# A GRU with a residual on one core: seven block products for eight in two gates, x products 64 columns wide, a tabled order

## The chip, the core and the metric

The kernel runs on one core of a Trainium2 chip. Such a core has a matrix engine (TensorE, PE in the profile; PEld is its weight loader), three elementwise engines (VectorE = DVE, ScalarE = ACT, GpSimd = POOL), and a sync engine (SP), which here issues most DMAs. Each engine works through its own instructions in order; semaphores hold them together. Data lie in SBUF on 128 partitions; TensorE writes to PSUM, whose banks GpSimd and the DMAs do not touch in this kernel. The metric is the device time of one execution in microseconds (us), as the median over runs.

## What is computed

A gated recurrent unit over 128 steps, 64 batch rows, 512 inputs and 512 hidden units, in float32, added to its input. After every fourth step but the last the state goes through one more layer.

```python
def step(h, inp):
    x_t, prop = inp
    comb = jnp.concatenate([x_t, h], axis=-1)
    z = jax.nn.sigmoid(comb @ Wz + bz)
    r = jax.nn.sigmoid(comb @ Wr + br)
    comb2 = jnp.concatenate([x_t, r * h], axis=-1)
    h_cand = jnp.tanh(comb2 @ Wh + bh)
    h_new = (1.0 - z) * h + z * h_cand
    h_next = jnp.where(prop, jnp.tanh(h_new @ Wp + bp), h_new)
    return (h_next, h_new)
...
return x + ys          # ys: all h_new, [64, 128, 512]
```

Each weight matrix has an upper half that meets x and a lower half that meets h. The x halves do not depend on the recurrence.

## The kernel before

**Recurrence.** The 64 batch rows are two halves of 32 (`S = 2`, `V = 32`). A gate of a half is eight matmuls: four blocks of 128 inputs, each with two matmuls of 256 columns (`products`, L213). The stationary operand is 32 columns wide (a block of the transposed state), so that each matmul takes one of TensorE's four 32-column groups: half h uses the groups 2h and 2h + 1. In PSUM, a partition stands for (half, column block, batch row), and the free axis for the other columns.

A step of a half (`half`, L777) runs: gate r; `crossed` (L239), which applies the sigmoid and brings the two column blocks onto the partitions of the state; r·h and its 32×32 transposes on VectorE (L794, L244); gate z; gate h on the transposed r·h; tanh; z·candidate, minus `keep` = (z − 1)·h (L831, L840); the transpose for the next step. ScalarE copies the x part of each gate from SBUF into PSUM ahead of the products (`seed`, L377), and the products add to it. The two halves are generators that give way to each other by the columns that they have issued, half 1 a lag of 700 columns behind half 0 (L868 to L880).

**x products.** From group 2 on (a group is four steps) the x products of four steps at once are block products by Strassen's scheme in Winograd's form, on two levels: seven for eight over (step pairs, input halves, column halves), and each of these again seven for eight. So a group takes 49 products instead of 64, each a pair of matmul rounds of 192 columns (three gates of 64). `batch` (L480 on) runs two outer products at once over five PSUM banks: ScalarE copies partial sums out (L484), VectorE adds them into a block `mb` (L501 to L511), and GpSimd adds those blocks, with the biases, into the steps' x parts `cp` (L542, L547), in the partition layout that the gates use. GpSimd also makes the sums of x (`four`, L307) and adds the new state to x for the output (L752). `fill` (L396) puts a number of x products, given per step by the tables `PLACES`, `HEAD` and `TAIL`, between the gates. Groups 0 and part of the last are plain products (`plain`).

**Order.** Within an engine it is the order in which this code issues: the two generators, the fills, and `behind_step` (L691) for the GpSimd sums, loads and stores. SyncE loads x twice in groups of four steps (`xr` for the output, `xs` for the products) and stores groups of four steps.

Of the kernel before, what the change touches and what calls it, by code (L numbers as in the profile page):

```python
# [11 lines left out]
U16 = mybir.dt.uint16  # L12
AF = mybir.ActivationFunctionType
ALU = mybir.AluOpType
PSUM = bass.MemoryType.PSUM


@with_exitstack
def kernel(
# [14 lines left out]
    nc = tc.nc  # L34
# [8 lines left out]
    K = D // P  # L43
    Q4 = 4
    CHUNK = 4
    FIRST = 2
    LAST = T // Q4 - 1
# [3 lines left out]

    const = ctx.enter_context(tc.tile_pool(name="const", bufs=1))
    xrp = ctx.enter_context(tc.tile_pool(name="xr", bufs=2))  # L60
    one = ctx.enter_context(tc.tile_pool(name="one", bufs=1))
    xtp = ctx.enter_context(tc.tile_pool(name="xt", bufs=2))
    mbp = ctx.enter_context(tc.tile_pool(name="mb", bufs=3))
    two = ctx.enter_context(tc.tile_pool(name="two", bufs=2))
# [3 lines left out]
    zeros = one.tile([P, 4 * J], BF16, tag="cq", name="zeros")  # L68
    nc.vector.memset(zeros, 0.0)
    ones = const.tile([1, V], F32, name="ones")  # L70
    nc.gpsimd.memset(ones, 1.0)

    wx = const.tile([P, K, 3, H], F32, name="wx")
    wh = [const.tile([P, K, H], F32, name=f"wh_{i}") for i in range(3)]
    wp = const.tile([P, K, H], F32, name="wp")

    tw = {n: const.tile([P, S, NQ, 3, J // 2], F32, name=f"tw_{n}") for n in (2, 3, 4, 5)}
    tf = {n: const.tile([P, NQ, 3, J // 4], F32, name=f"tf_{n}") for n in (1, 2, 3)}
    tt = const.tile([P, 7, 3, NQ, 3, J // 4], F32, name="tt")
    gates_in = (Wr, Wz, Wh)  # L80

    bias_row = tt.rearrange("p a b c d e -> p (a b c d e)")[0:1, : 3 * H].rearrange(
        "p (i n) -> p i n", i=3
    )
# [4 lines left out]
    def load_x(tile_, t0, n):  # L89
        for h in range(S):  # L90
            for q in range(NQ):
                nc.sync.dma_start(
                    out=tile_[part(q), 0:n, h, :], in_=x[ts(h, V), t0 : t0 + n, ts(q, J)]
                )

    def load_step(t, engs):
        for q in range(NQ):
            engs[q % len(engs)].dma_start(
                out=xr[0][part(q), t], in_=x[:, t, ts(q, J)].rearrange("(h b) j -> b h j", h=S)
            )  # L100

    def load_wx(wt, w, k0=0, k1=K):
        nc.sync.dma_start(  # L103
            out=wt[:, k0:k1, :], in_=w.rearrange("(p k) n -> p k n", k=K)[:, k0:k1]
        )

    def load_wh(wt, w, engs=(nc.sync,)):
        for q in range(NQ):
            engs[q % len(engs)].dma_start(  # L109
                out=wt[part(q)], in_=w[ts(q, P), :].rearrange("(k e) n -> e k n", e=V)  # L110
            )

    xr = {}

    def new_xr(g):
        xr[g] = xrp.tile([P, Q4, S, J], F32, tag="xr", name=f"xr_{g}")

    h_init = two.tile([P, S, J], F32, tag="h", name="h_init")
    bias_x = const.tile([P, C, S, 3, J // 2], F32, name="bias_x")
    bias_p = const.tile([P, S, J], F32, name="bias_p")  # L120
    new_xr(0)
    load_step(0, (nc.sync, nc.scalar))
    for k in range(0, K, 2):
        load_wx(wx[:, :, R, :], gates_in[R][:D], k, k + 2)
    for i in (Z, H_):
        load_wx(wx[:, :, i, :], gates_in[i][:D])

    load_step(1, (nc.gpsimd,))
    for i, b in enumerate((br, bh, bz)):
        nc.gpsimd.dma_start(out=bias_row[:, i, :], in_=b.rearrange("(o n) -> o n", o=1))  # L130
    for t in (2, 3):
        load_step(t, (nc.gpsimd,))
    for h in range(S):
        nc.gpsimd.dma_start(
            out=h_init[:, h, :],
            in_=h0[ts(h, V), :].rearrange("b (q j) -> q b j", q=NQ),
        )

    nc.gpsimd.tensor_copy(wh[R][0:1, 0, 0:1], wx[0:1, K - 1, H_, 0:1])
    for i in range(3):  # L140
        load_wh(wh[i], gates_in[i][D:], (nc.sync, nc.gpsimd))

    dummy = const.tile([1, 1], F32, name="dummy")
    nc.scalar.activation(dummy, ones[:, 0:1], AF.Sigmoid)

    xs = {}

    def load_xs(g):
        if g * Q4 < T:
            xs[g] = one.tile([P, Q4, S, J], F32, tag=f"xs{g % 2}", name=f"xs_{g}")  # L150
            load_x(xs[g], g * Q4, Q4)

    new_xr(1)
    load_x(xr[1], Q4, Q4)
    load_xs(2)
    load_wh(wp, Wp)
    for q in range(NQ):
        nc.sync.dma_start(
            out=bias_p[part(q)],
            in_=bp.rearrange("(o d c j) -> c o d j", o=1, d=2, c=2)[q % 2].broadcast_to(  # L160
                [V, S, J]
            ),
        )


    P_ = 3
    rec = [ps_c.tile([P, 2, 2, J], F32, name=f"rec_{n}") for n in ("0", "1", "z")]
    z = rec[2][:, 1]

    def gate_ps(i, h):  # L170
        return rec[2][:, 0] if i == Z else rec[h][:, 0 if i == R else 1]

    scratch = [ps_c.tile([P, 4 * J], F32, name=f"scratch_{n}") for n in "qraxy"]
    q_ps, r_ps, a_ps, *x_two = (
        s[:, : 3 * J].rearrange("p (m h v) -> p m h v", m=2, h=S) for s in scratch
    )
    q_bank, r_bank, a_bank, *x_banks = range(5)
    r_ = scratch[r_bank][:, 3 * J :]

    def quarters(v):  # L180
        return v.rearrange("p n (d c j) -> p c n d j", d=2, c=2)

    def spread(bank, rows, which):
        bank = bank.rearrange("p (i d j) -> p i d j", i=2, d=2)
        for h in range(S):
            for c in range(2):
                nc.tensor.matmul(
                    bank[part(2 * h + c), 0 : len(which)],
                    lhsT=ones,
                    rhs=quarters(bias_row[:, rows])[:, c],  # L190
                    start=True,
                    stop=True,
                )
        for j, i in enumerate(which):
            nc.scalar.copy(
                bias_x[:, :, :, i, :].rearrange("p n d u -> p d n u"),
                bank[:, j].rearrange("p d (n u) -> p d n u", n=C),
            )

    bias0 = bias_x[:, 0]  # L200
    bias_d = const.tile([P, S, 3, J // 2], F32, name="bias_d")

    def idle(n):
        for i in range(n):
            nc.tensor.matmul(
                rec[i // NQ % 3].rearrange("p a d n -> p (a d n)")[part(i % NQ)],
                lhsT=zeros[:, :V],
                rhs=zeros,
                start=True,
                stop=True,  # L210
            )

    def products(ps, h, left, rhs, start=False):  # L213
        for c in range(2):
            nc.tensor.matmul(  # L215
                ps[part(2 * h + c)],
                lhsT=left,
                rhs=rhs(c),
                start=start,
                stop=True,  # L220
                skip_group_check=True,
            )

    def gate(i, h, lT, w):
        for k in range(K):
            products(gate_ps(i, h), h, lT[:, h, ts(k, V)], lambda c: quarters(w)[:, c, k])
            yield S * J

    def product(ps, h, lT, w, k, start=False):
        c0, s0 = divmod(k, C)  # L230
        products(
            ps.rearrange("p (d j) -> p d j", d=2),
            h,
            lT[:, c0, s0 * B + h * V : s0 * B + (h + 1) * V],
            lambda c: quarters(w)[:, c, k],
            start,
        )

    def crossed(dst, h, i, func):  # L239
        for d in range(2):  # L240
            nc.scalar.activation(dst[ts(d, 2 * V)], gate_ps(i, h)[ts(h, 2 * V), d, :], func)  # L241

    def turn(dst, src):
        nc.vector.transpose(out=dst, in_=src)  # L244

    def new_T(tag, name):
        return two.tile([P, S, P], F32, tag=tag, name=name)

    xT = {}

    def join_x(g, i):
        if g * Q4 >= T:
            return
        if g not in xT:
            xT[g] = xtp.tile([P, Q4, C, P], F32, tag="xT", name=f"xT_{g}")
        src = xr[g] if g < FIRST else xs[g]
        nc.vector.transpose(
            out=xT[g][:, i].rearrange("p c (a h b) -> p h (c a) b", a=S, h=S),
            in_=src[:, i].rearrange("p h (e k) -> p h k e", k=K),
        )  # L260

    def outer(kb, nb, ka):
        return wx[:, kb * S + ka, :, :].rearrange("p g (q n u) -> p n q g u", q=NQ, n=C)[:, nb]

    OPERAND = {
        1: lambda ka: outer(0, 0, ka),
        2: lambda ka: outer(1, 0, ka),
        3: lambda ka: outer(1, 1, ka),
        4: lambda ka: tw[4][:, ka],
        5: lambda ka: tw[5][:, ka],  # L270
# [649 lines left out]
```

## Time and profile before

| | |
|---|---|
| median of 3 runs | 1277.04 us (1275.2 to 1277.14) |
| span of the profiled execution | 1273.0 us |
| difference of the median to that span | 4.0 us |
| mean granted TensorE clock | 0.997 of full speed |
| issues by SyncE | 767 DMAs |
| moved by DMA | 60.82 MB, mean 48 GB/s |

The span runs from the first to the last instruction of one profiled execution. A group line has: line, engine, operation, output<-inputs, output partitions × elements <- input, count | busy time in us, mean ns of one | idle time of the engine just before them, and what ended it. A matmul `128*32 128x256` has 128 rows, 32 stationary columns and 256 streamed columns. Every float32 matmul of the program is two records in the trace, each with its own weight load. Ends of matmuls are modelled by the profiler, starts are not. In a timeline a row has start, length, engine, line, operation and count; in brackets stands the engine's idle time before it.

### The profile page before, as it was taken

How to read it: one execution, taken by the hardware profiler on the slowest of the kernel's cores; microseconds unless marked ns; L12 is line 12 of the kernel's file. 1: busy time of each engine (PE TensorE's matmuls, PEld its weight loads, DVE VectorE, ACT ScalarE, POOL GpSimd, SP SyncE). 2: the span in 40 equal slices, each digit the busy share in tenths (PEclk: the TensorE clock that was granted, in tenths of full speed). 3: DMA queues.
4: the chain of work that ended last, by engine and by line, in shares of the span. 5: the costliest groups of instructions: out<-in, count | busy, mean ns of one | idle time of the engine just before them, and what ended most of it. 6: DMA issues, size and time to landing. Idle time of an engine off the chain costs nothing.

```text
span 1273.0 us, 60669 instructions
## 1 busy us (share of the span) xinstructions
PE 1255.9 (99%) x25954; PEld 1150.3 (90%) x25954; DVE 800.4 (63%) x2153; ACT 835.5 (66%) x2685; POOL 906.0 (71%) x1053
## 2 busy tenths in 40 slices
PE   7899999999999999999999999999999999999998
PEld 4699999999999999999999999999999999999885
DVE  2765666666666666666666665666666666666544
ACT  1356666766666666676666667666666666666665
POOL 8788767777677786777687677776777777677530
PEclk9999999999999999999999999999999999999999
DMA  8302212102121111211111121111111112111010
GB/s 233 76 19 53 52 41 60 40 24 49 53 53 36 36 47 42 53 36 44 49 32 53 46 59 37 29 43 53 53 37 37 48 39 52 37 52 35 4 50 21
DMA packets 112212, 60.82 MB, mean 48 GB/s; under 512 B 12776, under 2 KB 108520, under 8 KB 111944
## 3 DMA queue, kind: packets, MB, share of 16 engines
q1 hardware_dynamic: 110532, 54.71, 16.5%
q8 instruction: 205, 3.36, 1.1%
q0 software_dynamic: 1120, 2.11, 0.7%
q14 instruction: 63, 0.52, 0.1%
q10 hardware_dynamic: 292, 0.13, 0.0%
HBM read 40.11 MB, written 16.78 MB: 45 GB/s over the span
## 4 chain that ended last, share of the span: by engine, by line
PE 95%; DMA 2%; DVE 1%; issue 1%; SPq 0%; ACT 0%; POOL 0%; POOLq 0%; DVEq 0%
PE rec L215 43%; PE rec_z L215 16%; PE scratch_r L215 14%; PE scratch_q L215 10%; PE scratch_a L215 5%; PE scratch_x L215 4%; PE scratch_y L215 4%; DMA wh<-in_L_cond_Wh_dram 1%; DMA wx<-in_L_cond_Wh_dram 1%; DVE tw L292 0%; DVE tw L293 0%; DVE tw L291 0%; SPq L109 0%; ACT rec_z L241 0%; SPq L103 0%
## 5 line engine op out<-in xcount | busy, mean ns | idle before, releaser
L215 PE MATMUL rec<-wh,rhT 128*32 128x256 f32 x4096 | 373.2, 379 | 0.0
L215 PE MATMUL rec<-wh,hT 128*32 128x256 f32 x3072 | 281.1, 381 | 4.9 <-DVE hT L244 4.7
L215 PE MATMUL rec_z<-wh,hT 128*32 128x256 f32 x3072 | 280.0, 379 | 0.1
L215 PEld LDWEIGHTS rec<-wh,rhT 128*32 128x32 f32 x4096 | 241.2, 110 | 23.4 <-ACT scratch_r L241 1.3
L241 ACT ACTIVATE scratch_r<-rec 64x128 f32<-64x128 f32 x512 | 128.0, 250 | 136.0 <-PE rec L215 68.1
L380 ACT COPY rec<-cp 64x256 f32<-64x256 f32 x512 | 189.8, 371 | 23.6 <-DVE cp L418 4.2
L215 PEld LDWEIGHTS rec<-wh,hT 128*32 128x32 f32 x3072 | 175.0, 110 | 27.3 <-ACT rec L380 6.4
L215 PEld LDWEIGHTS rec_z<-wh,hT 128*32 128x32 f32 x3072 | 184.8, 110 | 7.3 <-issue 0.6
L241 ACT ACTIVATE rec_z<-rec_z 64x128 f32<-64x128 f32 x512 | 128.0, 250 | 93.7 <-PE rec_z L215 81.6
L241 ACT ACTIVATE c<-rec 64x128 f32<-64x128 f32 x512 | 139.3, 272 | 60.1 <-PE rec L215 48.9
L215 PE MATMUL scratch_r<-tw,s 128*32 128x192 f32 x1392 | 166.0, 326 | 0.0
L752 POOL TENSOR_TENSOR xr<-xr,h 128x256 f32<-128x256 f32 x127 | 93.2, 734 | 89.6 <-DVE h L840 89.6
L542 POOL TENSOR_TENSOR mb<-mb,mb 128x768 f32<-128x768 f32 x58 | 106.3, 1833 | 66.4 <-DVE mb L511 66.4
L542 POOL TENSOR_TENSOR cp<-mb,mb 128x768 f32<-128x768 f32 x76 | 139.2, 1832 | 18.7 <-ACT scratch_r L241 9.4
L542 POOL TENSOR_TENSOR cp<-mb 128x768 f32<-128x768 f32 x46 | 84.3, 1834 | 59.7 <-ACT rec_z L380 58.3
L810 DVE SCALAR_TENSOR_TENSOR keep<-rec_z,h 128x256 f32<-128x256 f32 x96 | 40.8, 425 | 123.6 <-ACT rec_z L241 122.5
L484 ACT COPY cq<-scratch_q 128x384 f32<-128x384 f32 x212 | 102.3, 482 | 19.4 <-PE scratch_q L215 17.8
L501 DVE TENSOR_TENSOR cx<-scratch_r,cx 128x384 f32<-128x384 f32 x106 | 58.5, 552 | 74.3 <-PE scratch_r L215 40.3
L215 PE MATMUL scratch_q<-tt,s 128*32 128x192 f32 x928 | 101.9, 326 | 0.0
L215 PEld LDWEIGHTS scratch_r<-tw,s 128*32 128x32 f32 x1392 | 90.7, 110 | 7.7
L507 DVE TENSOR_TENSOR mb<-scratch_q,cx 128x384 f32<-128x384 f32 x106 | 58.8, 555 | 58.8 <-ACT cq L484 58.8
L794 DVE TENSOR_TENSOR rh<-scratch_r,h 128x128 f32<-128x128 f32 x192 | 56.0, 292 | 62.3 <-ACT scratch_r L241 62.3
(168 smaller groups left out, 3718.0 us busy)
## 6 DMA issues: line engine op xcount, KB each, us to landing
out_dram<-xr SPq DMA_DIRECT2D x249, 64.0 KB, 1.8
xr<-in_x_dram SPq DMA_DIRECT2D x248, 64.0 KB, 2.1
xs<-in_x_dram SPq DMA_DIRECT2D x240, 64.0 KB, 2.1
wx<-in_L_cond_Wr_dram SPq DMA_DIRECT2D x2, 512.0 KB, 5.5
wx<-in_L_cond_Wz_dram SPq DMA_DIRECT2D x1, 1024.0 KB
wx<-in_L_cond_Wh_dram SPq DMA_DIRECT2D x1, 1024.0 KB
wp<-in_L_cond_Wp_dram SPq DMA_DIRECT2D x4, 256.0 KB, 6.2
wh<-in_L_cond_Wr_dram SPq DMA_DIRECT2D x2, 256.0 KB, 4.3
```

The source lines that it names most:

```text
L215: nc.tensor.matmul(ps[part(2 * h + c)], lhsT=left, rhs=rhs(c), start=start, stop=True, skip_group_check=True,)
L241: nc.scalar.activation(dst[ts(d, 2 * V)], gate_ps(i, h)[ts(h, 2 * V), d, :], func)
L380: nc.scalar.copy(gate_ps(i, h)[rows].rearrange("p d (c n) -> p d c n", c=C), G[t][rows, :, :, i, :].rearrange("p c d n -> p d c n"),)
L484: nc.scalar.copy(c[:, :nm], ps[:, :nm])
L501: nc.vector.tensor_add(T2[what][:, :nm], r_ps[:, :nm], T2[what][:, :nm])
L507: nc.vector.tensor_add(blocks(1, 1), runs(q_ps[:, :nm]), runs(T2[what][:, :nm]))
L542: nc.gpsimd.tensor_add(dst, a, b)
L752: nc.gpsimd.tensor_add(xr[g][:, j], xr[g][:, j], h_new)
L794: nc.vector.tensor_mul(rh[:, h, :], r_, h_old[:, h, :])
L810: nc.vector.scalar_tensor_tensor(out=keep, in0=z, scalar=1.0, in1=h_old, op0=ALU.subtract, op1=ALU.mult)
```

## The change

**Seven for eight in r and z (`gates_seven`, new).** In the steps 4 to 123 the two gates are taken as one 2×2 block product: rows are the early and the late batch half (`e`, `l`), inner blocks the first and second 256 hidden units, columns r and z. Seven products of [32 × 256] by [256 × 512] replace eight. Sums of the state's blocks (`sa`) are four 64-column subtractions on GpSimd in each step; sums of the weights are made once, into `s1`, `wt` (S2, S4) and over the first half of Wz. Products that go into several results land in one PSUM bank (`B_`, `E_`) and are added by VectorE, together with the x parts. The other steps use `gates_plain`; the lost half of Wz is loaded again before step 124.

**Layout of the gates.** A matmul of the recurrence now has 128 streamed columns. The four column groups take the four blocks of 128 hidden units of one half (partition = block and batch row), so that a half fills the whole array, and no `crossed` is needed. The lag of the halves is gone.

**x products in 64-column groups.** The stationary operand of an x product holds all 64 batch rows, where it held the 32 of one half, so a round is two matmuls on groups 64 wide, where it was four on groups 32 wide. Results are then not on the partitions of the gates: GpSimd adds into a stage `st`, and `place` moves each block with four DMAs of 98 KB into `cp`. `batch` copies a shared partial sum inside PSUM (bank to bank, on ScalarE) and lets the matmuls add to it, so that VectorE makes two additions per batch where it made five. Biases enter as seeds (`bias_s`), not as GpSimd additions.

**Order from a table.** The code first lists all operations with what they read and write (`Plan.add`), and `Plan.arrange` then issues them in an order decoded from a string, `ORDER`. It has 1047 places where TensorE goes from a stationary operand 64 wide to one 32 wide or back. x is loaded and stored per step and half, not in groups of four steps.

The diff, cut to its core:

```diff
-    def products(ps, h, left, rhs, start=False):
-        for c in range(2):
-            nc.tensor.matmul(
-                ps[part(2 * h + c)],
-                lhsT=left,
-                rhs=rhs(c),
...
-    LAG = 700
-    halves = [half(0), half(1)]
...
+    def arrange(self, table):
+        data, moves = zlib.decompress(base64.b85decode("".join(table.split()))), []
...
+        for n in moves:
+            op = self.ops[rest.pop(n)]
+            if not op.after <= given:
+                raise RuntimeError(f"{op.name} stands in front of what it waits for")
+            given.add(op.index)
+            line.append(op)
...
+    def product_k(ps, lT, w, ks, start, reads=(), writes=(), banks=""):
+        def emit():
+            for n, (kl, kw) in enumerate(ks):
+                for q in range(NQ):
+                    dst, right = ps[part(q)], w[:, kw, ts(q, J)] if w is not None else s1(kw)[:, q]
...
+                    mm(dst, lT[:, ts(kl, V)], right, start and n == 0)
...
+    def gates_seven(t):
...
+        seed(cn(R_), xpart(t, R, 1), gx[R][1], [("R", 0)], "r")
+        product_k(B_, e, wh[R], first, True, reads=he + wk(R, 0, 1), writes=[("B", 0), ("E", 0)], banks="+b")
+        plus(cn(A_), cn(B_), xpart(t, R, 0), [("B", 0)] + gx[R][0], [("A", 0)], "b +e")
+        product_k(A_, e, wh[R], second, False, reads=he + [("A", 0)] + wk(R, 2, 3), writes=[("A", 0)], banks="+e")
+        reset(t, 0)
+        s(0, l[:, :B], e[:, :B], he + hl)
+        s(1, l[:, B:], sa[:, 0], hl + [("sa", t, 0)])
+        product_k(R_, l, S4, [(2, 0), (3, 1)], False, reads=hl + [("R", 0), ("T", 0, 4)], writes=[("R", 0)], banks="+r")
...
+        el("act", 128, lambda: nc.scalar.copy(c2_(t), R_), [("R", 0)], [("c2", t)], "r", main=True)
+        p(E_, "E", 0, None, [("T", 0, 1)])
+        p(B_, "B", 1, S2, [("T", 0, 2)])
+        plus(c2_(t), E_, c2_(t), [("E", 0), ("c2", t)], [("c2", t)], "b")
+        plus(R_, B_, c2_(t), [("B", 0), ("c2", t)], [("R", 0)], "b +r")
+        s(2, l[:, B:], l[:, :B], hl)
+        s(3, e[:, B:], sa[:, 1], he + [("sa", t, 1)])
+        reset(t, 1)
+        p(B_, "B", 2, wh[Z][:, 0:KH], [("T", 0, 3)])
+        plus(cn(c3_(t)), cn(E_), xpart(t, Z, 1), [("E", 0)] + gx[Z][1], [("c3", t)], "b")
+        plus(zz[:, 1], B_, c3_(t), [("B", 0), ("c3", t)], [("z", 0, 1)], "b +z")
+        p(B_, "B", 3, wh[Z][:, KH:K], wk(Z, 2, 3))
+        plus(cn(zz[:, 0]), cn(B_), xpart(t, Z, 0), [("B", 0)] + gx[Z][0], [("z", 0, 0)], "b +z")
...
+                    def unit(left=left, right=right, m=m, first=first):
+                        for c in range(2):
+                            mm(ps[bank][ts(c, B), m].rearrange("p d (g u) -> p d g u", g=3),
+                               left, right[:, c::2], first)
...
+        product("q", 1, not any(bias))
+        copy(ps["a"], ps["q"], [key["q"]], [key["a"]], "q +a")
+        seeded("r", 1, 4)
+        product("r", 5, not any(bias))
+        copy(c5, ps["r"], [key["r"]], [("c5", n)], "r")
+        product("q", 6, False)
+        product("a", 2, False)
+        copy(block(0, 0), runs(ps["a"]), [key["a"]], blocks(0, 0), "a")
+        copy(ps["x"], ps["q"], [key["q"]], [key["x"]], "q +x")
+        copy(q2, ps["q"], [key["q"]], [("q2", n)], "q")
...
+    def place(g, a, nb, n):
+        for h in range(S):
+            for d in range(S):
+                load(
+                    "sp",
+                    lambda h=h, d=d: nc.sync.dma_start(
+                        out=cp_(2 * g + a)[ts(d, B), nb, :, h].rearrange("p b g u -> p b (g u)"),
+                        in_=st_(n)[h::2, :, d].rearrange("p b g u -> p b (g u)"),
+                    ),
...
+    plan.close()
+    for op in plan.arrange(ORDER):
+        op.emit()
```

More of the change, by code (lines that the diff above doesn't have):

```diff
@@ L71, with new @@
[L71 to L79, printed above, removed]
+    def new(name, shape, dtype=F32):
+        return const.tile(shape, dtype, tag=name, name=name)
@@ L119 @@
[L119 to L130, printed above, removed]
@@ L168 @@
[L168 to L181, printed above, removed]
@@ L224, in gate @@
[L224 to L259, printed above, removed]
+    def mm(dst, lhsT, rhs, start):
+        nc.tensor.matmul(dst, lhsT=lhsT, rhs=rhs, start=start, stop=True, skip_group_check=True)
@@ L361, in lhs @@
         if j in (1, 2):
[L362 removed]
+            ap, k = rows_[0]
+            return ap[:, ts(j - 1, B)], [k]
         if j == 4:
[L364 to L383 removed]
@@ L868 @@
[L868 to L880 removed]
+            ap, k = rows_[1]
+            return ap[:, ts(1, B)], [k]
+        ap, k = s({5: 0, 6: 1, 7: 2, 3: 3}[j])
@@ new lines, with idle @@
+    idles = [0]
+    def idle(n, reads=(("zeros", 0),), writes=()):
+        for _ in range(n):
+            i = idles[0]
+            idles[0] += 1
+            bank = (ae, rl, zz)[i // NQ % 3]
+            add("pe", 0.22, lambda bank=bank, i=i: nc.tensor.matmul(
+                bank.rearrange("p a n -> p (a n)")[part(i % NQ)], lhsT=zeros[:, :V], rhs=zeros,
+                start=True, stop=True), reads, writes or [("bits", 0)], rank=1e6)
+    idle(42)
+    for t in range(Q4):
+        join(t)
@@ new lines, with spread @@
+    spread_key = take("r")
+    spread_ps = scratch["r"][:, 0:3]
+    def spread():
+        for i in range(3):
+            for q in range(NQ):
+                nc.tensor.matmul(spread_ps[part(q), i], lhsT=ones[:, :V], rhs=bias_row[:, i, ts(q, J)],
+                                 start=True, stop=True)
+    add("pe", 0.6, spread, [("ones", 0)] + [("row", 0, i) for i in range(3)],
+        [spread_key, ("row_free", 0)], "+r")
+    el("act", 384, lambda: nc.scalar.copy(
+        bias_x.rearrange("p c i u -> p i c u"), spread_ps.rearrange("p i (c u) -> p i c u", c=C)),
+       [spread_key], [("st", -2)], "r")
```

1476 lines of the change are left out of this document (872 added, 604 removed), and 4 rows, old and new, of the table RINGS.

## The prediction

> **What bounds the kernel now.** I read the page first, then the busy time by stretch, then the chain of work that ended last, then single instructions.
>
> ```profile
> span 1273.0 us, 60669 instructions
> ...
> PE 1255.9 (99%) x25954; PEld 1150.3 (90%) x25954; DVE 800.4 (63%) x2153; ACT 835.5 (66%) x2685; POOL 906.0 (71%) x1053
> ...
> PE 95%; DMA 2%; DVE 1%; issue 1%; SPq 0%; ACT 0%; POOL 0%; POOLq 0%; DVEq 0%
> ```
>
> ```profile
> core 0: us, PE busy (x) PEld busy (x) DVE busy (x) ACT busy (x) POOL busy (x), PEclk, DMA share, GB/s
> 0.00:32.00 32.00, 25.53 (x366) 12.99 (x370) 6.53 (x17) 6.28 (x18) 25.93 (x42) 0.95 0.90 232
> 32.00:150.00 118.00, 113.25 (x2358) 103.21 (x2353) 79.01 (x188) 66.48 (x213) 93.11 (x103) 0.99 0.22 54
> 150.00:1140.00 990.00, 990.00 (x20759) 925.80 (x20754) 640.90 (x1735) 676.68 (x2172) 728.20 (x851) 1.00 0.17 43
> 1140.00:1273.00 133.00, 127.16 (x2494) 108.29 (x2486) 73.90 (x214) 86.05 (x285) 58.72 (x60) 1.00 0.12 30
> ```
>
> TensorE ends everything: 95% of the chain, and not one idle moment between 150 and 1140 us. A busy TensorE could still be a waiting one, so I check it against its own columns. The next two fences, chain of waits and timeline, give the period of eight steps and the time of one round, that is of the matmuls that run at once in the array's column groups.
>
> ```profile
> 235.12 0.99 PE rec L215 x16
> 312.16 0.99 PE rec L215 x16
> ...
> 1005.79 0.99 PE rec L215 x16
> 1082.84 0.99 PE rec L215 x16
> ```
>
> ```profile
> 601.12 0.36 PE L215 MATMUL scratch_q<-wx,o 128*32 128x192 f32 x2
> 601.28 0.36 PE L215 MATMUL scratch_q<-wx,o 128*32 128x192 f32 x2
> ...
> 601.93 0.36 PE L215 MATMUL scratch_r<-tf,s 128*32 128x192 f32 x2
> 602.10 0.41 PE L215 MATMUL rec<-wh,rhT 128*32 128x256 f32 x2
> ```
>
> Six rounds of 192 columns take 602.10 − 601.12 = 0.98 us, 0.1633 us each. For 256 columns I use three blocks from the head (32 records on four column groups, so eight rounds); the other rows are for later.
>
> ```profile
> 9.49 1.93 PE L215 MATMUL scratch_a<-wx,xT 128*32 128x256 f32 x32
> 11.35 1.06 PE L187 MATMUL scratch_x<-tt,ones 1*32 1x512 f32 x8
> 12.24 0.61 PE L187 MATMUL scratch_r<-tt,ones 1*32 1x256 f32 x8
> 12.78 1.93 PE L215 MATMUL scratch_q<-wx,xT 128*32 128x256 f32 x32
> 14.53 1.91 PE L215 MATMUL scratch_a<-wx,xT 128*32 128x256 f32 x32
> 16.25 1.91 PE L215 MATMUL scratch_r<-wx,xT 128*32 128x256 f32 x32
> 17.98 1.91 PE L215 MATMUL scratch_x<-wx,xT 128*32 128x256 f32 x32
> ```
>
> (17.98 − 14.53) / 16 = 0.2156 us a round. A gate of one step is 16 matmuls, each two records, on four groups: 8 rounds. Eight steps have 26 gates (r, z, h, and the extra product every fourth step) and 98 x products of two rounds: 26 × 8 × 0.2156 + 98 × 2 × 0.1633 = 44.8 + 32.0 = 76.8 us. The chain shows 77.04 and 77.05. So the steady part is column time with nothing added, and fewer columns are worth their full time there, as long as nothing else takes over.
>
> **The columns removed.** The built order of instructions gives the counts. Before: 6640 matmuls of 256 columns on the hidden state, 6020 of 192 and 288 of 256 on x. After: 12,320 of 128, 3052 of 192 that now fill two column groups of 64, and 384 of 128. In rounds before: 3320 × 0.2156 + 3010 × 0.1633 + 144 × 0.2156 = 715.8 + 491.5 + 31.0 = 1238.3 us. The remaining 34.7 us of the span are loads at the start, hand-offs there and at the end.
>
> A round of 128 columns stands nowhere in the trace. From below it is half of 256, 0.1078; from above the straight line through 192 and 256, 0.2156 − 2 × 0.0523 = 0.1110. I take 0.109, between these near neighbours. After: 6160 × 0.109 + 3052 × 0.1633 + 192 × 0.109 = 671.4 + 498.4 + 20.9 = 1190.7 us (1183.1 to 1203.5). That is **−47.6 us** (−55.2 to −34.8). In one step seven products of 4 rounds replace 16 rounds for r and z: 3.05 us for 3.45.
>
> **What is added on the other engines.** Durations:
>
> ```profile
> L241 ACT ACTIVATE c<-rec 64x128 f32<-64x128 f32 x512 | 139.3, 272 | 60.1 <-PE rec L215 48.9
> L484 ACT COPY cq<-scratch_q 128x384 f32<-128x384 f32 x212 | 102.3, 482 | 19.4 <-PE scratch_q L215 17.8
> L542 POOL TENSOR_TENSOR mb<-mb,mb 128x768 f32<-128x768 f32 x58 | 106.3, 1833 | 66.4 <-DVE mb L511 66.4
> L244 DVE STREAM_TRANSPOSE rhT<-rh 128x128 f32<-128x128 f32 x256 | 79.8, 312 | 8.7
> L840 DVE TENSOR_TENSOR h<-rec_z,keep 128x128 f32<-128x128 f32 x254 | 74.0, 291 | 15.8 <-POOL cp L542 0.5
> L547 POOL TENSOR_TENSOR mb<-mb,bias_x 128x768 f32<-128x768 f32 x34 | 62.3, 1831 | 28.3 <-DVE mb L511 28.3
> L507 DVE TENSOR_TENSOR mb<-scratch_q,cx 128x384 f32<-128x384 f32 x106 | 58.8, 555 | 58.8 <-ACT cq L484 58.8
> L547 POOL TENSOR_TENSOR mb<-mb,bias_d 128x768 f32<-128x768 f32 x30 | 55.0, 1834 | 23.8 <-DVE mb L511 23.8
> L311 POOL TENSOR_TENSOR s4r<-xT 128x64 f32<-128x64 f32 x29 | 9.5, 327 | 0.0
> ```
>
> Per step, from the stretch 150 to 1140 (990 us = 102.8 steps of 9.63 us). VectorE: 640.9 / 102.8 = 6.2 us; six more 128-column additions (+6 × 0.29) and three 384-column ones fewer per batch at 0.875 batches a step (−2.6 × 0.555) make 6.5, some 7 with the gaps between them. GpSimd: 728.2 / 102.8 = 7.1; four 64-column subtractions (+1.3) against the 34 + 30 bias additions that go (64 × 1.83 / 120 = −1.0) make 7.4. ScalarE stays near its 6.6: three evacuation additions of VectorE become copies of 0.48, and whole-width activations replace two half-width ones of 0.27. Against a step of 9.63 − 0.4 = 9.2 us that is 76, 80 and 72%: none becomes the bound.
>
> The 496 DMAs that carry x blocks to the steps' rows raise SyncE from 767 to 1288 issues:
>
> ```profile
> 602.07 4.77 SPq L92 DMA_DIRECT2D xr<-in_x_dram  x8
> ...
> out_dram<-xr SPq DMA_DIRECT2D x249, 64.0 KB, 1.8
> ```
>
> At 4.77 / 8 = 0.60 us an issue that is 770 us, 62% of the time. They add 496 × 98 KB = 49 MB to a DMA share of 0.17, and their landing (1.8 us in the row) lies inside the two steps, 18 us, for which a block's buffer stands free. An issue that waits for its sum or its buffer holds the later loads and stores in the same queue; in the built order those stand at least 11 us of TensorE's work ahead of their use, and nine in ten of the carried blocks 5.9 us or more. On the path: nothing. Without that lead each late block would stop a ScalarE seed, and with it a gate, by about 2 us.
>
> **The new waits.** Before, the two batch halves ran a lag apart and covered each other. Now the late half's r needs products that mix both halves, so cover can only come from x products.
>
> ```profile
> 707.05 0.29 DVE L794 TENSOR_TENSOR rh<-scratch_r,hprop 128x128 f32<-128x128 f32 x1 [0.19 <-ACT scratch_r L241]
> 707.38 0.31 DVE L244 STREAM_TRANSPOSE rhT<-rh 128x128 f32<-128x128 f32 x1
> 707.95 0.41 PE L215 MATMUL rec<-wh,rhT 128*32 128x256 f32 x2
> 708.42 0.41 PE L215 MATMUL rec_z<-wh,hpT 128*32 128x256 f32 x2
> 708.87 1.09 ACT L241 ACTIVATE rec_z<-rec_z 64x128 f32<-64x128 f32 x4 [0.49 <-PE rec_z L215]
> ```
>
> A result reaches ScalarE 0.45 us after the last 256-column matmul starts (708.87 − 708.42), some 0.24 after its columns are in. The late half's loop is then: two GpSimd subtractions 0.65, product 0.44 and 0.24, addition 0.33, sigmoid 0.27, multiplication 0.33, transpose 0.31, to TensorE at most 0.26 (707.95 − 707.69), h product 0.87 and 0.24, tanh 0.27, multiplication, subtraction and transpose 0.93: 5.1 us of a step of 9.2. The 12.25 x products a step (1470 / 120) bring 12.25 × 0.327 = 4.0 us to lay into it. In the built order most hand-offs have enough: between the h product of the early half and its next use stand about 4 us. Some are short: in 11 of the 120 steps at most one 0.44 us product stands between the first product of r and the matmul that waits for VectorE's addition to it, which takes 0.24 + 0.29 + 0.1 = 0.63. I add **+10 us** for such places, 0.08 us a step; below, −8 if the start loses less than now; above, +25, 0.2 us in each of 120 steps.
>
> Sum: 1273.0 − 47.6 + 10 = 1235.4 for the profiled execution. The median of the runs, 1277.04, is 4.0 above that span, so **1239 us**, own range 1214 to 1267.
>
> **The row against it.** In the head rows above, the tile changes twice, from 128 rows to 1 and back. The block at 9.49 should have been followed at 9.49 + 8 × 0.2156 + 0.02 = 11.24; the next starts at 11.35. After 12.24 two rounds should end at 12.67; the next starts at 12.78. The block at 12.78 takes 1.75 where its neighbours take 1.72. So a change cost 0.11 us plus 0.02, and no semaphore is named for it. The Trainium skill (TensorEngine Tiling (Array Packing), Key Properties) says that changing the tiling mode, not just the tile, drains TensorE; the two places agree with it, and its list of modes counts 128×64 and 128×32 as different ones. By it every change between x products and gates would pay.
>
> **The rivals.**
>
> 1. *Each change of tile width empties the array.* The old kernel only uses tiles 32 wide; the new one goes between 64 and 32 wide 1047 times. At 0.11 to 0.13 us: 115 to 136 us; the 10 us of short hand-offs vanish under it: 1239 − 10 + 125 = about **1355 us**, slower. For: the two rows. Against: those change the height, where sums leave the array at another row, not the width, and at 601 to 602 us column groups start matmuls at different times without waiting for each other. It decides from 0.05 us a change. 30%.
> 2. *The waits take the place of the columns.* One place: the four GpSimd subtractions of a step stand in order behind 1.83 us sums. If the late half's products wait 0.9 us at such a place in each of 120 steps, 108 us replace the 10: about **1337**. It decides from 0.4 us a step. For: GpSimd at 80%; against: 4 us of slack in the loop. 12%.
> 3. *Issue becomes the bound.* The fastest pace in the trace is four records in 0.1633 us, 0.041 each; a gate at 128 columns needs four in 0.109. The new kernel has 31,512 records: at 0.041 evened out 1286 us, some **1320** with start and end; unevened 1239 + 24,640 × 0.041 − 671 = 1578. Against: at 601 us the pace is set by columns, not by issue. 5%.
>
> **How the numbers follow.** Forecast 53%, rivals 30, 12 and 5%. A measurement of this kernel can tell about 0.2% from no change, 2.6 us. Nearly all of the forecast's own range lies below that band, and all rivals above: faster 52%, same 2%, slower 46%. The range runs from the forecast's low end, 1214, to rival 1's high end, 1239 − 10 + 136 = 1365; beyond it lie rival 3's upper part and the tail of rival 2.
>
> **What would show it.** Right: 32 records of 128 columns in 0.87 us, x products 0.163 us apart also beside gates, eight steps in 73.5 to 75 us. Rival 1: starts after a change of width 0.1 us late, and eight steps near 82. Rival 2: TensorE idle behind GpSimd's differences. Rival 3: 128-column rounds at 0.16. The forecast is wrong if the period of eight steps exceeds 77.

## The result and the profile after

The changed kernel takes **1416.28 us** (median of 4 runs, 1414.21 to 1418.23) beside 1276.62 us for the kernel before on the same chip: ratio 1.1093, 95% interval [1.1078, 1.1109]. It is slower by 140 us, and 177 us above the forecast of 1239 us. The page of the profile after:

```profile
span 1416.0 us, 73676 instructions
...
PE 1369.9 (97%) x31586; PEld 1059.5 (75%) x31586; DVE 836.7 (59%) x2567; ACT 670.2 (47%) x2063; POOL 936.0 (66%) x1476
...
PE 87%; SPq 5%; DMA 4%; issue 1%; POOL 1%; DVE 1%; ACT 1%; POOLq 0%; ACTq 0%; DVEq 0%
```

A busy share of 97% looks like the kernel before (99%), but the columns make only 1190.7 us. So TensorE is "busy" with time that is not columns. The same by stretch (length, then busy us of each engine):

```profile
0.00:32.00 32.00, 22.09 (x498) 15.66 (x498) 14.45 (x19) 4.06 (x10) 20.18 (x29) 0.89 0.57 168
32.00:60.00 28.00, 10.57 (x264) 9.03 (x264) 3.88 (x5) 0.66 (x2) 6.15 (x10) 0.65 0.28 98
60.00:1330.00 1270.00, 1260.46 (x28772) 972.08 (x28772) 773.11 (x2395) 628.75 (x1933) 872.29 (x1387) 0.99 0.26 77
```

Two things stand out: between 32 and 60 us TensorE is idle for 17.4 of 28 us, and from 60 us on it hardly ever is. Where the time goes in there, TensorE's timeline shows (start, length, form, count):

```profile
701.78 0.62 PE L402 MATMUL ps_r<-wh,rhT 128*32 128x128 f32 x16
702.22 0.62 PE L402 MATMUL ps_b<-wh,sa 128*32 128x128 f32 x16
702.77 0.55 PE L402 MATMUL ps_y<-tf,s 128*64 128x192 f32 x4
703.15 0.49 PE L402 MATMUL ps_y<-tw,s4r 128*64 128x192 f32 x4
703.47 0.49 PE L402 MATMUL ps_x<-tt,s 128*64 128x192 f32 x4
...
704.77 0.49 PE L402 MATMUL ps_y<-wx,s 128*64 128x192 f32 x4
705.10 0.49 PE L402 MATMUL ps_y<-tw,s4r 128*64 128x192 f32 x4
705.52 0.64 PE L402 MATMUL ps_b<-wh,hT 128*32 128x128 f32 x16
```

Read the starts, not the lengths. 16 records of 128 columns take 0.44 us (701.78 to 702.22), as forecast. The next 16 are followed after 0.55 us: 0.11 us late, and what follows has a tile 64 wide. Its first unit (one x product, two rounds of 192 columns) then takes 0.38 us (702.77 to 703.15) where the next ones take 0.32 and 0.33. Back again: 705.10 + 0.327 is 705.43, but the next start is 705.52. No semaphore is named at either place. Over all starts of the trace: 522 changes from 32 to 64 wide start 113 ns late (5th to 95th percentile 113 to 114), 522 from 64 to 32 start 100 ns late (99 to 100), and the first round after a change is 50 and 24 ns longer: 522 × 0.287 = 150 us in all. (The sum of everything that starts late at a change is 160 us; the rest of it is a few pauses of up to 3.4 us that happen to stand there.) The recorded starts after a change stand 70 to 71 ns before the modelled end of the last matmul, at either width, as if the array had to empty first. That is rival 1, in a cleaner form than the two head rows could show.

### The profile page after: what moved, and what is told of

The parts are those of the page before. It is cut to its first block, busy times and chain, and to the rows that moved or that the text cites. A ratio compares the mean times of both kernels' runs of the same rounds, so it can differ in the third digit from the quotient of the medians.

```text
span 1416.0 us, 73676 instructions
## 1 busy us (share of the span) xinstructions
PE 1369.9 (97%) x31586; PEld 1059.5 (75%) x31586; DVE 836.7 (59%) x2567; ACT 670.2 (47%) x2063; POOL 936.0 (66%) x1476
## 4 chain that ended last, share of the span: by engine, by line
PE 87%; SPq 5%; DMA 4%; issue 1%; POOL 1%; DVE 1%; ACT 1%; POOLq 0%; ACTq 0%; DVEq 0%
PE ps_b L402 19%; PE ps_e L402 15%; PE ps_r L402 15%; PE ps_x L402 11%; PE ps_q L402 11%; PE ps_y L402 10%; PE ps_a L402 5%; SPq L445 2%; DMA cp<-st 2%; SPq L427 1%; DMA xj<-in_x_dram 1%; PE ps_z L402 1%; SPq L790 1%; DMA out_dram<-xo 1%; POOL st L773 1%
## 5 line engine op out<-in xcount | busy, mean ns | idle before, releaser
L773 POOL TENSOR_TENSOR st<-mb,mb 128x768 f32<-128x768 f32 x77 | 140.7, 1827 | 27.9 <-ACT mb L740 26.1
L402 PE MATMUL ps_b<-wh,sa 128*32 128x128 f32 x3840 | 150.7, 275 | 0.9 <-DVE ps_z L983 0.5
L402 PE MATMUL ps_e<-wh,rhT 128*32 128x128 f32 x4096 | 138.0, 275 | 0.0
L402 PE MATMUL ps_r<-wh,rhT 128*32 128x128 f32 x4096 | 137.0, 274 | 0.2 <-issue 0.2
L885 DVE STREAM_TRANSPOSE hT<-h 128x128 f32<-128x128 f32 x318 | 98.5, 311 | 51.8 <-ACT h L932 41.5
L1062 POOL TENSOR_TENSOR xo<-xo,h 128x256 f32<-128x256 f32 x127 | 92.9, 731 | 53.8 <-DVE h L1045 51.3
L402 PEld LDWEIGHTS ps_e<-wh,rhT 128*32 128x32 f32 x4096 | 106.3, 109 | 28.5 <-issue 13.6
L402 PEld LDWEIGHTS ps_r<-wh,rhT 128*32 128x32 f32 x4096 | 110.6, 110 | 14.4 <-issue 6.0
L402 PEld LDWEIGHTS ps_b<-wh,sa 128*32 128x32 f32 x3840 | 103.6, 110 | 23.2 <-issue 16.4
L402 PE MATMUL ps_y<-tw,s 128*64 128x192 f32 x728 | 89.5, 335 | 0.0
```

Source lines behind the costliest of these rows:

```text
L402: nc.tensor.matmul(dst, lhsT=lhsT, rhs=rhs, start=start, stop=True, skip_group_check=True)
L773: el("pool", 768, lambda: nc.gpsimd.tensor_add(dst, a, b), reads, writes, rank=FOLD)
L885: add("dve", 0.345, lambda: nc.vector.transpose(out=dst, in_=src), reads, writes, main=True)
L1062: el("pool", 256, lambda: nc.gpsimd.tensor_add(xo(t), xo(t), h_(new_)), [("h", new_, 0), ("h", new_, 1), ("xo", t, 0), ("xo", t, 1)], [("x ...
```

## The experiments

All times are medians, each with its ratio to the kernel before on the same chip. My theory from this trace was: 150 to 160 us are changes of width, some 20 us the loads at the start, and the rest short hand-offs, that is waits of TensorE for a result of another engine.

**1. All tiles 32 wide.** Every 64-wide matmul of an x product becomes two 32 wide ones, on two column groups at once.

```diff
-                            mm(ps[bank][ts(c, B), m].rearrange("p d (g u) -> p d g u", g=3),
-                               left, right[:, c::2], first)
+                            for i in range(S):
+                                mm(ps[bank][ts(2 * c + i, V), m].rearrange("p d (g u) -> p d g u", g=3),
+                                   left[:, ts(i, V)], right[:, c::2], first)
```

> Every x product as four matmuls 32 wide in place of two 64 wide, in the same order, with the same results on the same partitions; changes of width fall from 1048 to 4. Theory (each change empties the array: in the trace of the changed kernel 113 and 100 ns late at the first new matmul, and 24 and 50 ns in the first round, 143 ns a change): 1416 - 1044 x 0.143 = 1267 us, up to 1280 if waits that the changes covered come out; eight steps in 74 to 75 us. Rival A (the order is too tight, chain waits set the time): the waits stay, 1350 or more. Rival B (issue bound: 37,700 matmul records where 31,500 were): above 1416.

Measured: 1341.46 us (1337.4 to 1344.29), ratio 1.0509 [1.0484, 1.0534]. The direction held and rival B fell, but only 75 of the expected 149 us came back; the time lies between the theory's 1267 to 1280 and rival A's 1350. The timeline shows that the changes are gone and units follow each other at 0.16 us a round, also beside gates:

```profile
700.82 0.57 PE L402 MATMUL ps_y<-tw,s 128*32 128x192 f32 x8
701.14 0.57 PE L402 MATMUL ps_y<-wx,s 128*32 128x192 f32 x8
701.47 0.68 PE L402 MATMUL ps_b<-wh,hT 128*32 128x128 f32 x16
702.07 0.64 PE L402 MATMUL ps_r<-wt,hT 128*32 128x128 f32 x16
```

So either a change costs half of what the starts say, or another wait had lain under them.

**2. Every third batch stays 64 wide** (546 changes; `if n % 3 == 1:` keeps the old matmul of experiment 1's diff).

> As e1_all32, but the x products of every third batch stay 64 wide: 546 changes of width instead of 1048, order unchanged. Theory: 1416 - 502 x 0.143 = 1344 us. Rival A: within 20 us of the changed kernel, or no line through 4, 546 and 1048 changes. Rival C (64-wide loads of the stationary operand are slow in themselves, not the change): the saving goes with the share of 64-wide products, two thirds of what e1_all32 saves, not half.

Measured: 1375.3 us (1369.43 to 1379.11), ratio 1.0771 [1.0737, 1.0805]: missed by 31 us. From 4 to 546 changes the time rises by 34 us, from 546 to 1048 by 41. The cost comes with the number, but again at half the price. The saving is 41 of 75 us, 55%, nearer to the 48% of the changes that went than to rival C's two thirds, though single runs spread by 10 us. The traces speak against rival C: away from a change a 64-wide round takes 0.163 us (705.10 − 704.77 = 0.33 for two, in the changed kernel), and a 32-wide one of experiment 1 the same (701.14 − 700.82 = 0.32 for two).

**3. The loads at the start as before.** SyncE's own timeline of the changed kernel says what the gap at 32 to 60 us waits for:

```profile
6.68 10.60 SPq L445 DMA_DIRECT2D wh<-in_L_cond_Wr_dram  x4
17.33 8.77 SPq L445 DMA_DIRECT2D wh<-in_L_cond_Wz_dram  x4
26.14 11.98 SPq L445 DMA_DIRECT2D wh<-in_L_cond_Wh_dram  x4
38.17 4.96 SPq L427 DMA_DIRECT2D xo<-in_x_dram  x2
43.26 9.86 SPq L427 DMA_DIRECT2D xj<-in_x_dram  x8
```

Each of the twelve `wh` loads holds the queue for 2 to 3 us (10.60 / 4 = 2.65), and the x of group 1 stands behind them. In the kernel before, such a load covers 32 partitions with four rows each; here it covers 128 with one. Only the loads' form is put back:

```diff
+            ) if over else nc.sync.dma_start(
+                out=dst[part(k)], in_=w[ts(k, P), :].rearrange("(k e) n -> e k n", e=V)
             ),
```

> The changed kernel with the hidden weights wh and wp loaded as before the change: each DMA fills 32 partitions with four rows of 512, not 128 partitions with one row each in four groups; x products stay 64 wide. Theory (those loads use few of the 16 DMA engines: share 0.28 and 100 GB/s from 20 to 60 us while SyncE is held 2 to 3 us per load): weights land by about 25 us instead of 39, and the time falls by 10 to 20 us, to 1396 to 1406. Rival D (the start is bound by the bytes or by the x loads behind the weights): under 4 us.

Measured: 1395.64 us (1394.94 to 1397.77), ratio 1.0939 [1.0923, 1.0955]; 20.6 us less, at the upper end of what I expected. The same rows of this kernel:

```profile
6.77 3.92 SPq L447 DMA_DIRECT2D wh<-in_L_cond_Wr_dram  x4
12.76 9.44 SPq L447 DMA_DIRECT2D wh<-in_L_cond_Wz_dram  x4
22.95 3.93 SPq L447 DMA_DIRECT2D wh<-in_L_cond_Wh_dram  x4
27.63 1.63 SPq L427 DMA_DIRECT2D xo<-in_x_dram  x2
30.01 7.86 SPq L427 DMA_DIRECT2D xj<-in_x_dram  x8
```

The x loads are issued 13 us earlier. Between 20 and 30 us the DMAs now move 222 GB/s, where the changed kernel's moved 106. The whole gain arises at the start: by TensorE's starts, matmul record 1200 comes 20.8 us earlier than in the changed kernel (61.5 for 82.3 us) and record 20,000 21.5 us. Some 1.6 us of it are not waiting but clock: between 77.8 and 81.2 us the clock granted to TensorE in the changed kernel was 0.50, and two groups of 32 and 64 records of 128 columns there take 1.71 and 2.53 us, where they take 0.90 and 1.74 in this run, at 1.00.

**4. Both (1 and 3).**

> e1_all32 and e3_loads together. Theory: both add, 1248 to 1262 us, faster than the kernel before the change. Rival A or B: slower than 1277.

Measured: 1320.01 us (1315.39 to 1325.29), ratio 1.0345 [1.0314, 1.0375], 58 us above the upper end of what I expected. The chain of waits and the waits of this kernel (us in total, times, longest; SPq is SyncE's queue) name the missing part:

```profile
PE 67%; DMA 11%; POOL 7%; DVE 4%; SPq 4%; issue 4%; ACT 2%; POOLq 0%; ACTq 0%; DVEq 0%
```

```profile
ACT ps_e L931 <- DMA cp<-st: 40.8, 28, 5.2
ACT ps_r L931 <- DMA cp<-st: 22.0, 15, 2.7
```

```profile
SPq L427 <- DMA out_dram<-xo: 162.0, 121, 4.9
```

```profile
130.13 0.59 SPq L427 DMA_DIRECT2D xj<-in_x_dram  x1
130.82 0.59 SPq L427 DMA_DIRECT2D xo<-in_x_dram  x1
131.51 2.67 SPq L793 DMA_DIRECT2D cp<-st  x4
...
132.85 0.57 ACT L931 COPY ps_e<-cp 128x128 f32<-128x128 f32 x2 [1.71 <-DMA cp<-st]
134.19 0.65 PE L402 MATMUL ps_r<-wt,hT 128*32 128x128 f32 x16 [1.35 <-DVE hT L888]
```

The seeds of ScalarE wait for blocks that the DMAs carry. In the same queue SyncE, which issues in order, stands 162 us behind `xo` loads (L427) that wait until the store out of the same buffer has landed; that this makes the blocks late is what experiment 5 tries. In the changed kernel itself the same two waits read:

```profile
ACT ps_e L928 <- DMA cp<-st: 16.7, 16, 4.4
...
ACT ps_r L928 <- DMA cp<-st: 11.0, 11, 1.9
```

While the changes of width slowed TensorE down, the blocks mostly came in time, although SyncE waited there for stores almost as long (153 us).

**5. The `xo` loads later in SyncE's order.** Experiment 4, with each load behind 4 us more of TensorE's work; nothing else moves.

```diff
+            if op.engine == "sp" and op.name[0] == "xo" and op.index in users and at[op.index] > 100.0:
+                t = max(at[op.index], min(at[op.index] + us, users[op.index] - 6.0))
...
-    for op in plan.arrange(ORDER):
+    for op in later(plan.arrange(ORDER)):
```

> e4_all32_loads with one thing moved in SyncE's order: the loads of x for the output (xo) stand 4 us of TensorE's work later, behind other DMAs, and at least 6 us ahead of their use. In e4_all32_loads these loads hold SyncE's queue 162 us in all, waiting for the store of the same buffer to land, and ScalarE and VectorE wait 70 us for the moved x blocks (cp) that stand behind them. Theory (the queue is what makes the blocks late, and the late blocks hold TensorE): the waits for the blocks halve and the time falls by 15 to 35 us, to 1285 to 1305. Rival E (the blocks are late through their own sums on GpSimd, or by landing): less than 5 us.

Measured: 1302.65 us (1301.67 to 1303.47), ratio 1.0214 [1.0199, 1.023]; 17 us less, as expected, and the wait for stores has shrunk from 162 to 23 us. The waits of ScalarE for blocks fell too, but not by half as expected, from 62.8 to 50.4 us, and others have grown in SyncE's queue:

```profile
SPq L1068 <- POOL xo L1065: 78.0, 35, 5.3
SPq L793 <- POOL st L776: 61.4, 33, 6.8
...
SPq L427 <- DMA out_dram<-xo: 23.0, 19, 4.9
```

```profile
ACT ps_e L931 <- DMA cp<-st: 32.5, 22, 2.8
ACT ps_r L931 <- DMA cp<-st: 17.9, 13, 2.5
```

**6. The stores 2.5 us later too, the loads 6.5 us.**

> As e5_late_xo with the xo loads 6.5 us later and the stores of the output 2.5 us later too, since stores hold the queue 55 us for GpSimd's additions. Theory: 3 to 15 us less than e5_late_xo. Rival E: as e5_late_xo within 5 us.

Measured: 1302.43 us, ratio 1.0218 [1.0201, 1.0235]: no difference to the fifth; the theory missed, and rival E's figure came. Moving the rest of the queue a little did not help.

**7. No moves at all.** Experiment 4 without the 496 DMAs.

```diff
-                    lambda h=h, d=d: nc.sync.dma_start(
-                        out=cp_(2 * g + a)[ts(d, B), nb, :, h].rearrange("p b g u -> p b (g u)"),
-                        in_=st_(n)[h::2, :, d].rearrange("p b g u -> p b (g u)"),
-                    ),
+                    lambda: None,
```

> e4_all32_loads without the 496 DMAs that move x blocks to the steps' rows; the x parts from step 4 on are then stale, the sums are still made. It bounds what the late blocks cost. Theory: TensorE's own columns (1191 us) and the start and hand-offs remain, 1240 to 1270 us, faster than before the change. Rival F (the waits between the products of one step, on VectorE and GpSimd, keep TensorE idle also without the DMAs): 1290 to 1315.

Measured: 1268.07 us (1267.92 to 1269.33), ratio 0.9946 [0.9931, 0.996]. So rival F fell, and the moves cost experiment 4 its 1320.0 − 1268.1 = 52 us. Experiment 5 got back 17 of these by SyncE's order alone. The other 35 went only when the moves went as a whole, with their issues, their 49 MB of traffic and the waits for them; on which of these they hang stays open. (The steps read old x parts here, so this is no usable kernel.)

**8. The x products straight on the rows of the gates.** If the moves cost 52 us, a layout that needs none should be faster than the kernel before: eight matmuls of 96 columns a unit for four of 192, GpSimd's sums written into `cp`. The matmuls of the edit:

```diff
-                        for c in range(2):
-                            for i in range(S):
-                                mm(ps[bank][ts(2 * c + i, V), m].rearrange("p d (g u) -> p d g u", g=3),
-                                   left[:, ts(i, V)], right[:, c::2], first)
+                        for h in range(S):
+                            for q in range(NQ):
+                                mm(ps[bank][part(q), m, h].rearrange("p (g u) -> p g u", g=3),
+                                   left[:, h::S], right[:, q], first)
```

> The fourth experiment's kernel with the x products written straight to the rows on which the steps read them: each unit is eight matmuls of 32 stationary columns (every second batch row) and 96 moving columns, the sums of GpSimd go directly into the block buffer (of which there are now three, in the place of two and the three staging buffers), and the 496 DMAs that moved the blocks are gone. Same columns, same sums, the order of the remaining work unchanged. Theory (late blocks and nothing else separate the fourth experiment's 1320 us from the 1268 us of the seventh, which left the moves out): 1255 to 1275 us, ratio 0.983 to 1.0, eight steps 75 to 77 us, and almost no wait of ScalarE's seeds that a DMA ends. Rival (the array cannot start shorter matmuls at the columns' pace: 3,052 units have eight records where they had four, so the program has some 49,900, and the shortest step from record to record that the traces show so far is 0.027 us, in the 128-column rounds of four in 0.109 us): eight records of a unit then take 0.218 us for 0.163 us, 168 us more, 1436 us; at half that excess 1352 us.

Measured: 1507.12 us (1502.1 to 1507.83), ratio 1.1811 [1.1795, 1.1828]: the slowest of all, and beyond the rival. Its page, and TensorE's weight loads where they paused:

```profile
PE 1321.4 (88%) x49922; PEld 1214.6 (81%) x49922; DVE 835.2 (56%) x2567; ACT 671.0 (45%) x2063; POOL 936.1 (62%) x1476
...
q8 instruction: 391, 6.41, 1.8%
...
PE 86%; issue 11%; POOL 1%; DVE 0%; DMA 0%; ACT 0%; POOLq 0%; DVEq 0%; ACTq 0%
```

```profile
1004.29 0.59 PEld L402 LDWEIGHTS ps_r<-wh,rhT 128*32 128x32 f32 x23 [0.38 <-issue]
1008.13 0.16 PEld L402 LDWEIGHTS ps_q<-wx,xT 128*32 128x32 f32 x8 [0.94 <-issue]
1011.85 0.19 PEld L402 LDWEIGHTS ps_x<-tt,o 128*32 128x32 f32 x8 [0.76 <-issue]
```

TensorE stops about every 3.8 us (3.84 and 3.72 between these rows) for no semaphore. By TensorE's starts, 127 or 128 records lie between most neighbouring pauses, whatever the shapes. The instruction queue's packets hold 6.41 MB / 391 = 16.4 KB, and 49,922 matmuls with as many weight loads are 390 times 256 instructions: about one packet for each pause. The trace's DMA records settle it: three packets of this queue end at 1002.84, 1006.67 and 1010.45 us, and the rows above start 1.45, 1.46 and 1.40 us later. Over the 307 pauses of more than 0.3 us between 120 and 1400 us, TensorE goes on 1.23 to 1.57 us after the end of a packet (5th to 95th percentile). TensorE waits for its instructions.

**9. 64 wide, quick loads, no moves** (experiment 3 with the edit of experiment 7). This puts the question of experiments 1 and 2 without the moves.

> The third experiment's kernel (x products 64 columns wide with their 1,047 changes of tile width, wh and wp loaded as before the change) without the 496 DMAs that move the blocks, so that from step 4 on the steps read old x parts: the seventh experiment with the changes of width put back. Theory (a change costs 0.14 us wherever nothing else waits; the first experiment got back only 75 us for 1,044 changes because the late blocks had lain under them): 1268 us and 1,044 x 0.14 = 1400 us or a little less, 1375 to 1405, and so hardly below the third experiment's 1396 us. Rival (a change is worth the 0.072 us that the first experiment got back, whatever the trace shows as its delay): 1343 us.

Measured: 1386.16 us (1385.69 to 1387.28), ratio 1.0858 [1.084, 1.0876]. The theory holds, the rival falls by 43 us. Experiments 9 and 7 differ in the width alone, so the changes cost 1386.2 − 1268.1 = 118 us.

**10. Half the columns in five of seven products, the same number of matmuls.** It changes products 2, 3, 4, 6 and 7 of experiment 8, and leaves out half of their results.

```diff
-                                   left[:, h::S], right[:, q], first)
+                                n = U4 if j in (1, 5) else U4 // 2
...
+                                   left[:, h::S], right[:, q, :, :n], first and h == 0)
```

> The eighth experiment's kernel with the moving columns of five of its seven block products halved, 48 for 96 (the other half of their results is left out), the number of matmuls unchanged. Theory (the eighth waits for PE's instructions: its pauses stand 127 to 128 records apart, and a packet of the instruction queue, 6.41 MB in 391 packets, holds 256 instructions, which is 128 matmuls with their 128 weight loads): the same 49,900 records need the same packets, so 1480 to 1515 us although 178 us of columns are gone (3,052 units x 5/7 x 0.082 us). Rival (short matmuls themselves are slow on the array): 1507 us less 178 us, about 1330 us.

Measured: 1507.56 us (1504.6 to 1510.52), ratio 1.1808 [1.1779, 1.1837]: not a microsecond less for 178 us of columns. The stretch from 120 to 1400 us (length, then busy us and records), first of experiment 8, then of this one for TensorE alone:

```profile
120.00:1400.00 1280.00, 1133.88 (x43360) 1045.32 (x43354) 723.56 (x2259) 590.06 (x1813) 821.75 (x1316) 1.00 0.13 39
```

```profile
120.00:1400.00 1280.00, 1010.94 (x43360) 1.00 0.14 39
```

The same 43,360 records in the same 1280 us, 3.78 us for 128 of them: instructions set the pace, not columns. Neither short matmuls nor their weight loads are slow in themselves: between two pauses of this run, groups of 16 records of 48 columns start at 1002.74 and 1002.91 us and the next group at 1003.08, 0.17 us for 16.

**11. Experiment 8 with the start flag on the first half only.** A matmul with this flag opens a sum in PSUM anew instead of adding to it.

> The eighth experiment's kernel with one thing changed: only the first batch half's opening matmul of a bank carries the start flag, where the eighth had it on both halves' (and so cleared the first half's opening product). Same instructions, same columns. Both theories: 1500 to 1510 us, as the eighth; the x parts are then the reference's.

Measured: 1510.92 us (1510.89 to 1510.95), ratio 1.1836 [1.1785, 1.1887]; the result of experiment 8 stands.

No version beat the kernel before; the only one below it, experiment 7, leaves the moves out and with them the right x parts.

## Why the prediction was wrong

Experiments 3, 4, 7 and 9 are the four corners of two causes, all with the quick loads:

| | blocks moved | not moved | cost of the moves |
|---|---|---|---|
| 64 wide, 1047 changes | 1395.6 | 1386.2 | 9.5 |
| 32 wide throughout | 1320.0 | 1268.1 | 51.9 |
| cost of the changes | 75.6 | 118.1 | |

From the forecast to the result: 1239 + 29 (start, hand-offs) + 118 (changes of width) + 9.5 (moves) + 20.6 (form of the `wh` loads) = 1416 us. The order of the steps matters, as the table shows: with the moves still there the changes cost 76, and at 32 wide the moves cost 52. Only the loads cost the same either way (20.6, and 21.5 between experiments 1 and 4). Of the 29, some 23 are hand-offs beyond the 10 that I had put (below); by difference, the other 6 lie in the start and the end.

- **The columns removed.** Right: 0.109 us a round of 128 columns (0.44 us for 16 records, four rounds), 0.163 beside gates. Experiment 7 lets the gain be seen, less what follows.
- **The step that failed: the choice between forecast and rival 1.** The sum put 1047 changes of width at nothing. I had the two head rows, and set them aside because they change the height of the tile and not the width. The runs show that the width alone does it: 113 and 100 ns late, and 50 and 24 ns in the first round, and nine in ten of the 1044 counted lie within 1 ns of these delays. The Trainium skill (TensorEngine Tiling (Array Packing), Key Properties) says that a change of tiling mode drains TensorE. By that rule a step between 32 and 64 wide pays each time; the trace agrees, at 0.14 us a change. Rival 1's 115 to 136 us was too small for the delays in the trace (150), while the time freed, 118, lies within it. That is partly luck: its price of a change was too low (0.11 to 0.13 us for 0.1435), and it let only 10 us of hand-offs vanish under the changes. Taking the changes away freed 118 of 150 us, and most of the other 32 came out as waits (see the new waits below).
- **The x-block DMAs, "On the path: nothing".** Failed, though little of it shows in the result: 9.5 us there, 52 once TensorE runs at the columns' pace. I checked each block's lead in TensorE's work, and counted the issues, but did not price the waits at the head of the queue: 162 us behind loads whose buffer still had a store under way (experiment 4). Taking these waits away gave back 17 of the 52 (experiment 5); the cause of the other 35 stays open. The fallback that I had named, a late block stops a ScalarE seed and a gate, is what the waits show, 1.5 us a time on average (40.8 / 28).
- **The new waits, +10 us.** Too small. TensorE's timeline has the extra product `wp` once in a chunk of four steps; two of its rows of experiment 7, which has neither changes nor moves, and two of the changed kernel:

```profile
399.40 0.87 PE L402 MATMUL ps_e<-wp,hT 128*32 128x128 f32 x24
...
1158.74 0.64 PE L402 MATMUL ps_e<-wp,hT 128*32 128x128 f32 x16
```

```profile
422.58 0.64 PE L402 MATMUL ps_e<-wp,hT 128*32 128x128 f32 x16
...
1261.06 0.65 PE L402 MATMUL ps_e<-wp,hT 128*32 128x128 f32 x16
```

  Twenty chunks lie between the two rows, ten times eight steps, so eight steps take (1158.74 − 399.40) / 10 = 75.9 us and (1261.06 − 422.58) / 10 = 83.8 us; the columns alone make 73.7. So hand-offs cost 2.2 us in eight steps, 0.28 us a step, some 33 us over 120 steps; my upper bound had been 0.2 a step. In the changed kernel 671 changes lie between its two rows, 67 in eight steps, 67 × 0.1435 = 9.6 us; 73.7 + 9.6 = 83.3 leaves 0.5 us for hand-offs, so the other 1.7 lie under the changes. The 83.8 us is beyond 77, which I had named as the sign of a wrong forecast, and near the 82 that I had named for rival 1.
- **The start.** I allowed for a gain of 8 us; the form of the new `wh` loads cost 20.6 instead (experiment 3). The built order shows these DMAs; I counted them and didn't price their form.
- **Rival 2** fell: in the result no wait of TensorE or its weight loads for GpSimd is longer than 0.6 us, and its subtractions `sa` hold them for under 4 us in all. **Rival 3** (0.041 us a record) fell here, since experiment 4 runs 37,690 records in 1313 us at 128-column rounds of 0.109 us; with 49,922 records its mechanism came true in experiment 8, at 0.030.

## What to carry to other kernels

Count how often TensorE goes from one tile width to another, and price it before the columns are counted: 0.14 us a time was worth more here than the columns saved, and splitting each stationary operand into the width that the neighbours use cost no column time here, though it takes twice the matmuls. Price a cause by experiments that switch both it and its neighbour: a wait can lie under another cost, and come out when that is taken away. Where a queue issues in order, look at what its oldest entry waits for, and where the number of matmuls grows, at the bytes of instructions.

## What the runs showed of the hardware

- A change between tiles 32 and 64 wide delays the next start by 113 ns (to 64) and 100 ns (to 32), with a spread of 1 ns; the next start stands 70 to 71 ns before the modelled end of the last matmul.
- TensorE's instructions came at no more than 128 matmuls with their weight loads in 3.78 us (experiments 8 and 10), in packets of 256 instructions, and TensorE went on 1.2 to 1.6 us after a packet's end; short stretches run faster: 16 records of 128 columns in 0.44 us, 0.027 us each. Experiment 7 has 34,064 records in 1120 us, 4.2 us for 128, close to that limit; its pauses mostly do not stand 128 records apart.
- A 256 KB load over 128 partitions with one 2 KB row each held SyncE's queue for 2.2 to 3.0 us, the same bytes over 32 partitions with four rows each about 1.0 us in two of three groups (3.92 / 4 and 3.93 / 4).
